# Longer due times in the order planner of a transformer kernel: sums through DRAM, inverses, division

## The chip, the cores and the metric

The kernel runs on one core of one Trainium2 chip. A core has five instruction streams that run in order, each on its own, and meet only at semaphores: PE (TensorE, matmuls, with its weight loads shown apart as PEld), DVE (VectorE), ACT (ScalarE), POOL (GpSimd) and SP (SyncE, which here only issues DMAs). The metric is the device time of one execution in microseconds. Three timed runs of the kernel before took 914.91, 919.50 and 925.57 us, median 919.5 us.

## The reference

The input x is 4 batches of 1,024 tokens with 256 channels, float32. Two layers follow, each added to its input.

```
x = x + attn(layernorm(x))            # 16 heads of 16, causal, ALiBi slopes, then w_proj
x = x + ffn(layernorm(x))
ffn(x): qkv = x @ in_proj.T           # attention over the 4 batches at one position, 16 heads
        h   = layernorm(x + attn @ out_w.T)
        e   = max(top2(softmax(h @ router_w.T)))   # one of 8 experts for each token
        return layernorm(h + gelu(h @ w1[e].T + b1[e]) @ w2[e].T + b2[e])
```

The softmax of the first layer is what this case is about: exp(scores) is multiplied with the values, a column of ones beside the values gives the sum of the exponentials, and the product has to be divided by that sum before the projection w_proj.

## The kernel before, in words

**Attention.** The queries are cut into 20 units (`units`, line 680 on). Units 0 to 11 are 256 queries of one batch each (chunks c = 0, 1, 2 for the four batches in turn), units 12 to 15 the seventh 128 of the queries of each batch, units 16 to 19 the eighth. For every unit four groups g of four heads are worked on in rounds over up to 512 columns of keys: `score` (scores on PE, exponentials on ACT, causal mask on POOL) and `weigh` (product with the values on PE, copied or added into the tile `yt`). There are 160 rounds; two rounds make a slot, so there are 80 slots.

**The way to the division.** The product comes out with channels on partitions, four heads to a tile, and row D of each head holds the sum. To bring sums and values into a shape in which one instruction divides, they go through DRAM: `weigh` writes `yt` to `y` (a DMA); `load_sums(u)` reads the sums back to 128 partitions; `invert(u)` takes their reciprocals on DVE and writes them to `r`; `load_y(u)` issues four DMAs that read `r`, repeated over the 16 channels of each head, into `su`, and the values into `yc`; `divide(u)` multiplies the two on DVE; `project(u)` multiplies with w_proj on PE, and DVE adds the result to x. All DMAs here but those of units 0 to 3's `y` are issued on SP's queue, as are the loads of keys (`fill_slots`), which wait until PE has read what they overwrite. `yc`, `su` and `inverse` have two buffers each. The last unit, 19, goes another way (`normalise`, `project_slots`) without DRAM.

**The second layer.** `front(i)` does all of it up to the routing for 128 positions of all four batches (i = 0 to 7); it may start when `project` of batch 3 has done its queries (`projected`: units 3, 7, 11 give fronts 0 to 5 in pairs, unit 15 gives front 6, the end of attention front 7). At most two fronts run at once during attention, in small steps that fill the space between rounds. When six fronts are placed, `tabulate_first` makes the first table: which tokens go to which expert in 18 tiles of 128. After attention the planner of the tail mixes front 7 (steps marked `last`) and what is left of the others with the tiles of the first table (`tile_step`: gather on POOL, two matmul stages, layernorm, scatter on POOL); then `tabulate_rest` makes the table of the other 20 tiles, and these are done.

**What sets the order.** The program is written out by a planner that keeps a model clock for PE, DVE and ACT (`time`, `busy`, `on_tensor`). Each slot p emits: scores of a round, `E_slot(2p)`, `D_slot(p)`, scores of the next round, the product of an earlier pair of rounds, `E_slot(2p+1)`. An E slot emits work without matmuls, a D slot work with matmuls. When the last product of unit u has been emitted, `attended(u, at)` puts the five steps on lists with the model time at which each is due, `at` plus a constant. An E or D slot pops what is due by PE's model time; so a step is never emitted inside its due time, but in the first slot that begins after it, and several steps that have come due are emitted together. The model clock knows nothing of DMAs, of waits between engines or of the granted clock: it gives the attention phase some 575 model us. At the end of attention whatever is still on the lists is emitted at once, ahead of `normalise(2)`, `normalise(3)`, `project_slots` and the tail.

The constants and where they are used (line 76; `attended`, line 2125, uses them):

```
SUMS_BY, INVERTED_BY, Y_BY, DIVIDED_BY, PROJECTED_BY = 3.0, 6.5, 9.0, 13.0, 14.0
```

The helper at line 587 emits every instruction of PE, DVE and ACT, so most rows carry L587; they are told apart by tile names. PSUM banks are shared between steps, so the matmuls of `project` appear under the names op, xtp, qkp, passed and router, always with the input wp,yc.

Of the kernel before, what the change touches and what calls it, by code (L numbers as in the profile page):

```python
# [72 lines left out]
D_SLOT = 10.0  # L73
SWITCH, COLUMN, EXP_AT_ALL, EXP, READ = 0.2, 1 / 600, 0.17, 1 / 1200, 0.7
AHEAD, EARLY_BY, ROOT, OF_D = 1.0, 0.2, 1.4, 0.35
SUMS_BY, INVERTED_BY, Y_BY, DIVIDED_BY, PROJECTED_BY = 3.0, 6.5, 9.0, 13.0, 14.0

EXP_ZERO = -126 * math.log(2.0)

# [2395 lines left out]
```

## Time and profile before

| | |
|---|---|
| profiled execution | 919.38 us, span 917.7 us from first to last instruction, granted PE clock 0.908 |
| busy in the span | PE 736.4 (80%), PEld 550.0, DVE 545.4 (59%), ACT 416.7, POOL 251.9 us |
| attention, some 40 to 730 us | 80 slots |
| first and last `divide` | 77.0 us, 728.2 us |
| tail, 730 to 918 us | PE busy 139.8, DVE 131.3, POOL 104.6 us |

A row of the trace names the engine, the instruction, the tiles written and read (out<-in), and the time; the views of waits give, for each pair, the idle time of an engine before an instruction and what ended it. "Stretch" tables give the busy time of every engine in one window. Timelines give the start, the duration and, in brackets, the idle time of the engine just before. SPq is SP's sequencer, which issues DMAs; a row there is the issue, not the transfer.

### The profile page before, as it was taken

How to read it: one execution, taken by the hardware profiler on the slowest of the kernel's cores; microseconds unless marked ns; L12 is line 12 of the kernel's file. 1: busy time of each engine (PE TensorE's matmuls, PEld its weight loads, DVE VectorE, ACT ScalarE, POOL GpSimd, SP SyncE). 2: the span in 40 equal slices, each digit the busy share in tenths (PEclk: the TensorE clock that was granted, in tenths of full speed). 3: DMA queues.
4: the chain of work that ended last, by engine and by line, in shares of the span. 5: the costliest groups of instructions: out<-in, count | busy, mean ns of one | idle time of the engine just before them, and what ended most of it. 6: DMA issues, size and time to landing. Idle time of an engine off the chain costs nothing. (4 is left out here: it accounts for less than half of the span.)

```text
span 917.7 us, 22503 instructions
## 1 busy us (share of the span) xinstructions
PE 736.4 (80%) x8917; PEld 550.0 (60%) x8917; DVE 545.4 (59%) x1316; ACT 416.7 (45%) x625; POOL 251.9 (27%) x360
## 2 busy tenths in 40 slices
PE   3995656987999989898886597987798889766983
PEld 2674444655656655565565565776576758655872
DVE  7433313665468767749745435477366768975763
ACT  1452333545446545545553445456346536222540
POOL 5441101212112211212211101012112324508885
PEclk9898778998999999999897898999799989878997
DMA  7444231433325322414252515337242282314430
GB/s 199 137 128 136 74 119 53 122 115 113 98 64 168 93 76 70 143 28 147 67 150 67 161 45 159 93 78 185 62 134 69 76 317 67 108 34 127 119 110 28
DMA packets 75219, 99.56 MB, mean 108 GB/s; under 512 B 19496, under 2 KB 58723, under 8 KB 74596
## 3 DMA queue, kind: packets, MB, share of 16 engines
q1 hardware_dynamic: 64576, 79.63, 29.3%
q0 software_dynamic: 4864, 14.16, 5.1%
q10 hardware_dynamic: 5668, 4.25, 1.5%
q8 instruction: 73, 1.20, 0.6%
q14 instruction: 38, 0.31, 0.1%
HBM read 61.55 MB, written 35.12 MB: 105 GB/s over the span
## 5 line engine op out<-in xcount | busy, mean ns | idle before, releaser
L587 ACT ACTIVATE p<-sk 128x1024 f32<-128x1024 f32 (+1 forms) x320 | 287.6, 939 | 229.3 <-PE sk L587 204.8
L986 POOL TENSOR_SCALAR_AFFINE_SELECT p<-p 128x512 f32<-128x512 f32 (+1 forms) x160 | 104.1, 655 | 505.6 <-ACT p L587 504.0
L587 PE MATMUL sk<-slots 32*128 32x128 f32 (+1 forms) x3456 | 184.9, 333 | 32.2 <-issue 11.0
L587 PEld LDWEIGHTS sk<-slots 32*128 32x128 f32 x3456 | 139.9, 192 | 79.5 <-issue 35.5
L587 PE MATMUL pv<-p,v 128*32 128x128 f32 (+1 forms) x3456 | 151.4, 324 | 8.4 <-ACT p L587 6.5
L587 PEld LDWEIGHTS pv<-p,v 128*32 128x32 f32 x3456 | 100.6, 114 | 48.6 <-issue 14.5
L587 DVE TENSOR_TENSOR yc<-yc,su 128x512 f32<-128x512 f32 (+1 forms) x19 | 11.4, 598 | 116.5 <-DMA yc<-y 116.5
L587 PE MATMUL qkvp<-w_in,ut 128*128 128x264 f32 (+1 forms) x224 | 76.5, 477 | 0.0
L587 PEld LDWEIGHTS qkvp<-w_in,ut 128*128 128x128 f32 x224 | 39.6, 190 | 27.0 <-issue 22.3
L587 PE MATMUL oe<-w,ge 128*128 (+1 forms) x152 | 44.0, 414 | 14.3 <-DVE given L587 6.0
L587 PE MATMUL op<-wp,yc 128*128 128x256 f32 x60 | 21.2, 500 | 42.0 <-DVE yc L587 31.2
L587 PE MATMUL qkp<-xt,wqk 128*128 128x256 f32 x208 | 51.7, 392 | 0.2 <-ACT p L587 0.2
L587 PE MATMUL hid<-mt,w 128*128 128x128 f32 x304 | 48.5, 298 | 3.5 <-DMA w<-in_w_dram 3.1
L1813 POOL DMA_INDIRECT given<-rows,rows x38 | 42.6, 1120 | 23.9 <-DVE at_t L587 13.9
L587 PEld LDWEIGHTS hid<-mt,w 128*128 128x128 f32 x304 | 43.3, 206 | 5.2 <-DMA w<-in_w_dram 3.4
L587 PEld LDWEIGHTS qkp<-xt,wqk 128*128 128x128 f32 x208 | 37.5, 189 | 9.7 <-issue 3.0
L1929 POOL DMA_INDIRECT out_dram<-o,out_rows x38 | 39.0, 1025 | 8.7 <-issue 6.1
L587 PEld LDWEIGHTS op<-wp,yc 128*128 128x128 f32 x60 | 13.5, 243 | 46.4 <-issue 32.2
L587 DVE TENSOR_TENSOR pr<-qkv 128x1024 f32<-128x1024 f32 x32 | 40.2, 1256 | 1.3 <-ACT qkv L587 1.3
L587 DVE TENSOR_TENSOR pv<-qkv,sc 128x1024 f32<-128x1024 f32 x32 | 40.4, 1263 | 0.1
L587 DVE COPY qkv<-qkvp 128x264 f32<-128x264 f32 x28 | 12.0, 431 | 47.3 <-PE qkvp L587 47.3
L587 DVE TENSOR_REDUCE sc<-pr 128x64 f32<-128x1024 f32 x32 | 39.0, 1220 | 1.1
(339 smaller groups left out, 1087.3 us busy)
## 6 DMA issues: line engine op xcount, KB each, us to landing
slots<-k SPq DMA_DIRECT2D x128, 80.0 KB
k<-kq SPq DMA_DIRECT2D x32, 256.0 KB
v<-v SPq DMA_DIRECT2D x16, 288.0 KB
v<-v SPq DMA_DIRECT2D x4, 1152.0 KB
x<-in_x_dram SPq DMA_DIRECT2D x16, 256.0 KB
y<-yt SPq DMA_DIRECT2D x16, 256.0 KB
rows<-x SPq DMA_DIRECT2D x32, 128.0 KB
slots<-k SPq DMA_DIRECT2D x64, 64.0 KB
```

The costliest lines, as they stand in the source:

```text
L587: ins = made(*args, **kwargs)
L986: nc.gpsimd.affine_select(blocks, blocks, pattern=[[0, 2], [0, size], [1, P]], compare_op=ALU.is_ge, fill=0.0, base=0, channel_multiplier=-1,)
L1813: nc.gpsimd.indirect_dma_start(out=self.hx, out_offset=None, in_=t.rows_of, in_offset=bass.IndirectOffsetOnAxis(ap=t.rows_[:, self.j:self. ...
L1929: ins = nc.gpsimd.indirect_dma_start(out=out.rearrange("t n c -> (t n) c"), out_offset=bass.IndirectOffsetOnAxis(ap=t.table.out_rows[:, t. ...
```

## The change

Five constants of the planner get larger. Nothing is added to the computation and nothing removed; the same functions are called with the same arguments, and the same instructions are emitted in another order.

```
-SUMS_BY, INVERTED_BY, Y_BY, DIVIDED_BY, PROJECTED_BY = 3.0, 6.5, 9.0, 13.0, 14.0
+SUMS_BY, INVERTED_BY, Y_BY, DIVIDED_BY, PROJECTED_BY = 7.0, 14.0, 18.0, 29.0, 31.0
```

Since `projected` puts the fronts on the queue, these also can start later.

## The prediction

> **What bounds the kernel now.** I read the page's busy times first, then the waits, then the timelines of one unit. PE is the busiest engine. With matmuls and weight loads merged, it is idle for 115 us between 60 and 730 us of the span and for 32 us in the tail (my union of the trace's records). So in attention it counts what PE waits for. The waits of DVE and PE (us in total, times, longest):
>
> ```profile
> DVE yc L587 <- DMA yc<-y: 116.5, 18, 14.5
> DVE inverse L587 <- DMA sums<-y: 45.6, 12, 7.4
> PE op L587 <- DVE yc L587: 31.2, 4, 9.3
> PE qkp L587 <- DVE yc L587: 17.7, 2, 12.9
> ```
>
> DVE stands still 162.1 us in 30 waits for the DMAs on the way to the division, and PE stands behind it. Unit 12 shows how; timelines of SP, DVE and PE:
>
> ```profile
> 517.87 0.37 SPq L1053 DMA_DIRECT2D r<-inverse  x1
> 520.53 0.60 SPq L1068 DMA_DIRECT2D su<-r  x1
> ...
> 522.44 0.57 SPq L1071 DMA_DIRECT2D yc<-y  x1
> ```
>
> ```profile
> 515.95 0.25 DVE L587 RECIPROCAL inverse<-sums 128x16 f32<-128x16 f32 x1
> 524.91 0.42 DVE L587 TENSOR_TENSOR yc<-yc,su 128x256 f32<-128x256 f32 x1 [8.71 <-DMA yc<-y]
> ```
>
> ```profile
> 515.00 1.17 PE L587 MATMUL sk<-slots 32*128 32x128 f32 x32
> 525.44 2.04 PE L587 MATMUL op<-wp,yc 128*128 128x256 f32 x4 [9.26 <-DVE yc L587]
> ```
>
> The division is DVE's very next instruction after the reciprocal: the model had passed 6.5, 9 and 13 us in one jump of its clock, and all three steps came out together. The real chain is r's issue and landing (517.87 to 520.53), four issues (to 523.01), 1.9 us of landing. PE has `project` next and waits 9.26 us. Adding up where PE's idle time overlaps these waits of DVE gives **74.6 us** of the 115; the rest is spread over keys, exponentials and copies.
>
> A second cost is the clock. Stretches, columns: length, then busy time (and instructions) of PE, PEld, DVE, ACT, POOL, then PEclk, DMA share, GB/s:
>
> ```profile
> 65.00:150.00 85.00, 49.55 (x496) 37.00 (x496) 23.19 (x64) 27.34 (x42) 13.05 (x20) 0.80 0.36 106
> 150.00:250.00 100.00, 90.03 (x906) 62.00 (x907) 58.06 (x120) 50.38 (x71) 21.63 (x27) 0.94 0.35 101
> 250.00:350.00 100.00, 90.96 (x912) 58.69 (x915) 68.37 (x160) 49.41 (x66) 19.04 (x21) 0.95 0.33 101
> ```
>
> Where the long waits lie, the clock is lowest. The trace's clock intervals are at full or half rate; PE works 64.3 us inside half-rate intervals that lie at these waits, and its 128x256 matmul of `project` takes 379 ns at best and 765 ns at worst.
>
> **What the change does, part by part.** It adds and removes no instruction; only places change. To find them I followed the planner's own sums for the kernel before (order, no chip time) and looked up, with the new constants and the same slot times, where each step falls; the new order moves those slot times a little.
>
> *Sums and reciprocal.* Before, 8 of 19 units emit `load_sums` and `invert` in one E slot; with 7 and 14, 2 do (units 3 and 12). Their wait is priced at 45.6 / 12 = 3.8 us of DVE. The other 17 have at least one round between; the 1.7 us from issue to reciprocal in unit 4 (175.8 to 177.5) fits there.
>
> *Reciprocal to division.* `invert` and `load_y` still fall together in 8 units, but then only SP waits, for r to land (2.7 us above); behind SP stand the loads of keys for the next unit, wanted a whole unit later. `load_y` and `divide` fall in one slot in 5 units before and in none after; 11 model us lie between, and attention runs 1.2 real us for each (690 / 575), so some 13 us against 2.6 us of issue and 2 to 4 us of landing (unit 4: last issue 181.3, division 185.7). So DVE finds its data there. What hides the way now is one to three rounds of attention; without that cover it is again 9 us a unit.
>
> *PE's idle time.* Of the 74.6 us I take 65: the two units that coincide keep up to 3.8 each, and PE will find another wait behind some of the others. Bounds 45 (4 in 10 of the gaps turn into waits for copies, such as the 47.3 us that DVE itself waits for qkvp) and 75.
>
> *The clock.* Between 0 and 32 us (half of 64.3). Some half-rate intervals at 290, 311 and 434 us have no long wait, so I take 15. The Trainium skill, TensorE: Matmul & The Clock Gate, section "Part 1: The HAM clock gate", says the ramp penalty is under 1% of a typical kernel's span; by it this term would be 9 us at most and the forecast 6 us later.
>
> *The end of attention.* Before, unit 18's division was emitted in the last E slot and waited 2.07 us at 728.17. Now `attended` at 546.9 of 562.8 model us puts `invert` in the last E slot and `load_y`, `divide` and `project` behind the last round, at once. Behind `divide` on DVE are two `normalise` and the add to x, behind `project` on PE the last projection and the tiles. From reciprocal to `project` unit 12 took 9.2 us, of which the last products cover some 2: **+7 us** (0 to 9).
>
> *Fronts.* `project` of units 3, 7, 11 and 15 moves from slots 11, 28, 51 and 69 to 14, 31, 54 and 71, so the fronts start 2 or 3 slots later. Front 6 and the first table are then 2 or 3 slots less far when attention ends. What stays for the tail, from the rows: about four pairs of pr and sc (1.26 + 1.22 us each) and the softmax between (about 2.6 us), so 12.5 us of DVE, with perhaps the table's last step. DVE is busy 81.54 of 100 us at 730 to 830, where it would lie, so between nothing and 12.5 us, and up to 12 more for the table; I take **+10 us**. Tiles of the first table start later by as much, and these fill PE beside front 7.
>
> *Buffers.* Units come at least 12 model us apart, so `load_y` of unit u+2 comes 42 or more after `attended(u)`, behind `project(u)` at 31 to 39: two buffers suffice nearly everywhere, at no cost.
>
> *Sum*, against the profiled execution's 919.4 us (1.7 over its span, and 0.1 under the median of the runs): 919.4 - 65 - 15 + 7 + 10 = 856.4, so **856 us**.
>
> **The rivals.**
> - *Half the gain.* PE's gaps go, but DVE's work that stood behind them then collides with the copies out of PSUM, which PE waits for; the clock gives nothing. For: DVE is 68% busy at 250 to 350. Against: it is 59% over the span and loses 162 us of waits. 919 - 40 + 7 + 10 = 896 us. Chance 0.16.
> - *A dearer tail.* The first table is not ready when attention ends, so no tile is gathered ahead and the first ones wait for weights behind the layer's. +35 instead of +10 in the tail: 881 us. For: the table's five steps came in slots 75 to 77 of 80, so three slots later touches the end. Chance 0.17.
> - *Cheaper.* The full 75, 30 from the clock, and a tail that takes the rest beside front 7: 919 - 75 - 30 + 7 + 3 = 824 us. Chance 0.12.
> - *Slower.* The fronts slip more than the slots say, so that the table starts only in the tail. Then the 13 tiles that the tail does beside front 7 come behind it, at POOL's 1.12 + 1.03 + 0.75 us each (gather, scatter, root), 38 us, and all of front 6 with its some 40 us of DVE, +7: 85 us against 80 of gain, and with the last of front 5 some 930 us. It decides if fronts slip by five slots or more; I count 2 or 3. Chance 0.06.
> - *Nothing happens*, because the slots are so coarse that the steps come out together as before. The count of slots says no: 0 of 19 divisions in the slot of their loads. 919 us. Chance 0.03.
>
> **How the numbers follow.** Forecast 856 us (840 to 872) has 0.46. The range goes from the cheaper case to half the gain with a few us to spare: 822 to 903. A measurement of this kernel can tell about 1% from no change. Faster by more than 1%: 0.46 + 0.16 + 0.17 + 0.12 = 0.91; within 1%: 0.03; slower: 0.06.
>
> **What will show it.** In the profile after, DVE's waits for yc's and sums' DMAs fall from 162 us to under 30, PE's waits for yc to under 10, and PEclk at 65 to 150 us rises over 0.90. The last `divide` comes at 650 to 670 us instead of 728 and has several us of idle time before it. From it to the end are 190 to 210 us (189.5 before), with more of pr, sc and the table in it. I am wrong if PE's idle time stays above 80 us in attention, or if the tail grows by more than 35 us.

## The result, and the profile after

The changed kernel takes 837.26 us (834.96 to 839.94, 4 runs) against 919.25 us before: a ratio of 0.910, 95% interval 0.904 to 0.917. Measured again beside other kernels it was 0.914 (0.911 to 0.917). The forecast was 856 us, with 822 to 903 as its range. The result lies inside that range, 19 us below the forecast and 3 us below the narrower band of 840 to 872.

The page of the changed kernel, its first lines and the granted clock by slice:

```profile
span 837.1 us, 22503 instructions
...
PE 719.4 (86%) x8917; PEld 540.2 (65%) x8917; DVE 544.6 (65%) x1316; ACT 416.6 (50%) x625; POOL 251.1 (30%) x360
...
PEclk9799889998999999998999999999997699978997
```

The number of instructions is the same and DVE's busy time nearly so (545.4 us before). PE is 17 us less busy (736.4 before) with the same matmuls. The waits that the prediction showed, in the profile after (us in total, times, longest):

```profile
DVE inverse L587 <- DMA sums<-y: 40.9, 8, 11.0
...
DVE yc L587 <- DMA yc<-y: 28.2, 7, 8.6
...
PE op L587 <- DVE yc L587: 5.8, 1, 5.8
...
PE router L587 <- DVE yc L587: 5.2, 1, 5.2
```

The wait for yc has gone from 116.5 to 28.2 us; one more of 5.1 us before a division is put down by the view to a load of keys. PE's wait for the division, in four rows 31.2 + 17.7 + 7.6 + 7.2 us before, is two waits: 5.8 us at the end of attention and 5.2 us at unit 1. The wait for the sums is nearly what it was; more on that below. Unit 12 again, timelines of SP, DVE and PE of the changed kernel:

```profile
461.20 0.38 SPq L1053 DMA_DIRECT2D r<-inverse  x1
461.67 3.27 SPq L939 DMA_DIRECT2D slots<-k  x4
465.25 0.60 SPq L1068 DMA_DIRECT2D su<-r  x1
...
467.15 0.57 SPq L1071 DMA_DIRECT2D yc<-y  x1
```

```profile
459.88 0.24 DVE L587 RECIPROCAL inverse<-sums 128x16 f32<-128x16 f32 x1
...
474.74 0.42 DVE L587 TENSOR_TENSOR yc<-yc,su 128x256 f32<-128x256 f32 x1
```

```profile
478.21 1.03 PE L587 MATMUL vp<-wp,yc 128*128 128x256 f32 x4
```

From reciprocal to division it is now 14.9 us instead of 9.0, but DVE works in between, and neither it nor PE's projection has a wait in brackets. The projection's four matmuls take 1.03 us, where they took 2.04 after the 9 us gap.

By stage (my union of the records of matmuls and weight loads, from 40 us on; attention ends with the last product of exponentials and values):

| kernel | attention ends | PE idle in attention | PE busy in attention | tail | span |
|---|---|---|---|---|---|
| before | 727.7 | 116.2 | 571.5 | 190.0 | 917.7 |
| after | 630.0 | 44.4 | 545.6 | 207.1 | 837.1 |
| waits_gone | 615.0 | 31.7 | 543.3 | 188.2 | 803.2 |
| after_waits_gone | 602.0 | 23.0 | 539.0 | 199.9 | 801.9 |
| division_late | 624.6 | 39.4 | 545.2 | 200.2 | 824.8 |
| division_18 | 649.7 | 57.4 | 552.3 | 202.1 | 851.8 |
| all_shifted | 731.7 | 124.0 | 567.8 | 212.1 | 943.8 |
| fronts_late | 747.1 | 138.9 | 568.1 | 208.1 | 955.2 |
| fronts_early | 664.2 | 65.9 | 558.3 | 202.4 | 866.6 |
| sums_early | 624.1 | 41.1 | 543.0 | 205.7 | 829.8 |
| sums_early_end | 625.8 | 40.8 | 545.0 | 199.8 | 825.5 |

The kernels other than before and after are told below. In span, the change saves 80.6 us: 71.8 of PE's idle time and 25.9 of its busy time in attention, less 17.1 that the tail grew.

### The profile page after: what moved, and what is told of

It reads as the page before. It is cut to its first block, busy times and chain, and to the rows that moved or that the text cites. A ratio compares the mean times of both kernels' runs of the same rounds, so it can differ in the third digit from the quotient of the medians.

```text
span 837.1 us, 22503 instructions
## 1 busy us (share of the span) xinstructions
PE 719.4 (86%) x8917; PEld 540.2 (65%) x8917; DVE 544.6 (65%) x1316; ACT 416.6 (50%) x625; POOL 251.1 (30%) x360
## 5 line engine op out<-in xcount | busy, mean ns | idle before, releaser
L587 PE MATMUL sk<-slots 32*128 32x128 f32 (+1 forms) x3456 | 181.7, 328 | 21.2 <-DVE kq L587 10.0
L587 PEld LDWEIGHTS sk<-slots 32*128 32x128 f32 x3456 | 138.1, 188 | 64.9 <-issue 26.8
L587 PE MATMUL pv<-p,v 128*32 128x128 f32 (+1 forms) x3456 | 144.5, 314 | 10.4 <-ACT p L587 4.6
L587 PEld LDWEIGHTS pv<-p,v 128*32 128x32 f32 x3456 | 96.7, 111 | 48.3 <-issue 8.3
L587 PE MATMUL qkvp<-w_in,ut 128*128 128x264 f32 (+1 forms) x224 | 79.1, 489 | 0.0
L587 PE MATMUL qkp<-xt,wqk 128*128 128x256 f32 x208 | 54.4, 407 | 0.2 <-ACT p L587 0.2
L587 PEld LDWEIGHTS qkp<-xt,wqk 128*128 128x128 f32 x208 | 39.6, 200 | 11.1 <-issue 3.3
L587 ACT COPY qkv<-qkvp 128x512 f32<-128x512 f32 (+1 forms) x28 | 15.3, 555 | 58.5 <-PE qkvp L587 43.9
L587 PEld LDWEIGHTS oe<-w,ge 128*128 128x128 f32 x152 | 28.0, 205 | 17.8 <-DVE given L587 5.7
L587 PE MATMUL vp<-wv,xt 128*128 128x256 f32 x128 | 35.3, 423 | 0.0
```

The lines of the kernel that those rows point to most:

```text
L587: ins = made(*args, **kwargs)
```

## The experiments

**What are the waits worth in all?** The order of before, with what makes DVE wait taken away (two places of the edit; the projection then reads `dv`):

```
-        nc.vector.reciprocal(inverse[:, :width], sums[u])
+        nc.vector.reciprocal(inverse[:, :width], minus_half.to_broadcast([P, width]))
...
-        nc.vector.tensor_tensor(yc, yc, su, ALU.mult)
+        nc.vector.tensor_tensor(dv, flat[:, :n], flat[:, :n], ALU.mult)   # flat is wp_sb
```

> The order of the kernel before, instruction for instruction, with all its DMAs, but the reciprocal reads a constant, and the division multiplies parts of the constant tile wp (384 columns in place of 512, 256 for small units) into a tile of its own that the projection reads: neither waits for a DMA. It leaves out the division by the sums. Theory (the 75 us of PE's idle time under DVE's waits, and 15 to 25 us of clock, are all there is): PE idle between 60 us and the end of attention falls from 115 to some 45 us, PE's busy time falls by 15 to 25 us with the same instructions (the clock alone), tail 189 us as before, time 820 to 834 us. Rival (the gaps turn into other waits): PE idle 80 us, 860 to 880 us.

Measured: 806.79 us, a ratio of 0.883 (0.879 to 0.888), 109 us less, more than both theories allowed. The result of this kernel is not the reference's, since it leaves out the division by the sums, and its divisions are a little narrower; the matmuls are the same. Stretches of this kernel from 40 us to the end of its attention, and of the kernel before (columns as in the prediction):

```profile
40.00:615.00 575.00, 542.78 (x7873) 396.66 (x7871) 392.48 (x883) 338.03 (x465) 126.68 (x186) 0.99 0.42 123
```

```profile
40.00:728.00 688.00, 570.82 (x7870) 413.38 (x7869) 392.10 (x882) 338.20 (x464) 124.58 (x184) 0.91 0.35 103
```

The same matmuls in the same order take 28 us less of PE's time, at a clock of 0.99 for 0.91; idle time falls by another 84.5 us, from 116.2 to 31.7; the tail does not move. So 28 of the 112.7 us that attention gained are the clock. The trace's clock intervals bear this out: PE works 74.5 us inside half-rate intervals of attention before and 13.1 in this kernel, and half of the difference is 31 us. It shows too in the matmuls that stand right behind a wait; groups of the kernel before and of this one:

```profile
L587 PE MATMUL op<-wp,yc 128*128 128x256 f32 x60 | 21.2, 500 | 42.0 <-DVE yc L587 31.2 <-ACT p L587 5.8 <-DVE u L587 3.6
L587 PE MATMUL xtp<-wp,yc 128*128 128x256 f32 x32 | 11.2, 509 | 7.6 <-DVE yc L587 7.6
```

```profile
L587 PE MATMUL op<-wp,dv 128*128 128x256 f32 x60 | 17.2, 425 | 4.0 <-DVE dv L587 3.3 <-ACT yt L587 0.7
L587 PE MATMUL xtp<-wp,dv 128*128 128x256 f32 x32 | 7.8, 386 | 0.0
```

**Which of the five constants?** Only the last two late, then all late with the old distances from loads to division:

```
+SUMS_BY, INVERTED_BY, Y_BY, DIVIDED_BY, PROJECTED_BY = 3.0, 6.5, 9.0, 29.0, 31.0     # division_late
+SUMS_BY, INVERTED_BY, Y_BY, DIVIDED_BY, PROJECTED_BY = 7.0, 14.0, 18.0, 22.0, 23.0   # all_shifted
+SUMS_BY, INVERTED_BY, Y_BY, DIVIDED_BY, PROJECTED_BY = 3.0, 6.5, 9.0, 18.0, 19.0     # division_18
```

> Constants 3.0, 6.5, 9.0 as before, 29.0 and 31.0 as after: sums, reciprocal and loads early, only division and projection late. Theory A (PE loses its time because division and projection are emitted with the loads or within a slot of them): DVE's wait for yc falls under 25 us, its wait for the sums stays near 45 us since 8 units still emit read and reciprocal together, but PE does not see it, because the projection stands 22 model us behind; PE's waits for yc under 10 us; time 832 to 850 us, as the changed kernel. Rival B (what counts is that the whole chain starts later behind the last product, when SP's queue has come along): only half the gain, 870 to 890 us.

> Constants 7, 14, 18, 22, 23: the chain starts as late as in the changed kernel, but from loads to division and projection only 4 and 5 model us, as before. Theory A: in 7 units the division is again in the slot of its loads and in most others one E slot behind, so DVE waits 70 to 110 us for yc, PE 40 to 60 us for DVE; 885 to 910 us. Rival B: 840 to 855 us.

Measured: division_late 832.68 us, ratio 0.911 (0.908 to 0.914), the whole gain; all_shifted 947.28 us, 1.037 (1.033 to 1.042), slower than before. Theory A holds and rival B falls in both. But all_shifted lies outside theory A's numbers too (885 to 910 us, 70 to 110 us of DVE's waits): it came out slower than before. Its projections, and with them the fronts, are 9 model us later, which costs time where waits are left (fronts_late below); how much of it that explains was not measured. The waits of all_shifted, and then the only wait on this way that is left among the 60 longest of division_late:

```profile
DVE yc L587 <- DMA yc<-y: 141.9, 17, 14.3
PE op L587 <- DVE yc L587: 39.3, 7, 9.3
...
PE qkp L587 <- DVE yc L587: 36.1, 5, 15.4
```

```profile
DVE inverse L587 <- DMA sums<-y: 65.4, 13, 12.5
```

In division_late DVE stands 65.4 us before reciprocals, more than in the kernel before, and PE idles 39.4 us, less than in the changed kernel. Of PE's idle time from 60 to 625 us only 7.3 lie under these waits. Here they are nearly free. That PE's next need of DVE is mostly far behind the reciprocal is the likely reason.

> Constants 3.0, 6.5, 9.0, 18.0, 19.0: the division 9 model us behind its loads in place of 4, the projection 5 later than before in place of 17. If 9 model us (11 real) cover the loads, waits for yc stay under 30 us, fronts come hardly later, the first table is ready at the end of attention and the tail is 190 to 195 us: 815 to 828 us. If the full 20 model us of division_late are needed, waits for yc are 50 us and more: 840 to 870 us.

Measured: 858.77 us, 0.944 (0.939 to 0.949), by time the second case. DVE waits 38.2 us for yc's loads, and once more 5.3 us that the view puts down to a load of keys, so its waits lie between the two cases. With 4, 9 and 20 model us from loads to division the ratio is 1, 0.944 and 0.911: the longer the distance, the larger the gain. 9 is too short although 9 model us are 11 real ones and from the first load to the division are some 6 (unit 4 before: 179.4 to 185.7). In all these kernels the projection moved together with the division, so what each of the two distances is worth alone was not measured.

**What do later fronts cost?** In the kernel before, and then the changed order without waits:

```
-            queue.extend(front(PC * c + i + k, fact, 1, False) for k in range(size))
+            due_E.append((time["PE"] + 17.0, 0.0, lambda: queue.extend(
+                front(PC * c + i + k, fact, 1, False) for k in range(size)
+            )))
```

> The kernel before, but fronts get on the queue 17 model us after the projection that frees them: the price of the change's later fronts alone, with all waits for the division left as they are. Theory: front 6 and the first table are 2 slots less far when attention ends; the tail grows from 189 to 198 to 205 us, attention loses 5 to 8 us of work, net +3 to +10 us: 922 to 930 us. Rival (a dearer tail, first table not ready): 940 us and more. Rival (the work moved fits beside front 7): 912 to 919 us.

> The changed constants, with the same cut as waits_gone: reciprocal of a constant, division of parts of wp, so neither waits for a DMA (the division by the sums is left out). Beside waits_gone it shows the price of the later fronts when no wait for the division is left on either side. Theory (in fronts_late 19 us came into attention because later fronts leave the waits less covered, and 18 into the tail because front 6 and the first table are less far): without waits attention is 5 to 12 us shorter than in waits_gone (work moved out), the tail 15 to 19 us longer; 808 to 818 us. Rival (later fronts cost attention time by themselves): 830 us and more.

Measured: fronts_late 957.51 us, 1.047 (1.042 to 1.051), by far worse than my theory; after_waits_gone 802.86 us, 0.882 (0.877 to 0.888), the same as waits_gone at 0.883 and a little under its theory. In fronts_late the time is that of the rival with the dearer tail, and its condition is met (the first table is made at 744 to 768 us, behind the end of attention), but the tail holds only 18 of the 42 us. In both kernels the tail grows, by 18.1 and 11.7 us, with 13 and 11 us more of DVE's work in it. They differ in attention. Without waits it loses 13 us along with the work that moved. With waits it grows by 19.4 us: PE's idle time under DVE's waits goes from 74.6 to 93.5 us. So later fronts cost nothing where no wait is left, and 42 us where the waits are left. That the front's steps, which had stood between loads and division, no longer cover the waits is how I read it; which steps of which unit, I have not taken apart.

**Could the fronts be had early and the waits gone?** As division_late, with shorter times where fronts hang on the projection:

```
+        if units[u][0] % B == B - 1 or u == last_unit - 1:
+            late_by = (3.0, 6.5, 9.0, 16.0, 17.0)
```

> As division_late (3.0, 6.5, 9.0, 29.0, 31.0), but the units of batch 3, whose projection lets fronts start, and unit 18 divide at 16 and project at 17. Theory: 8 units of batch 3 and 18 keep waits of some 2 to 4 us each, the other 11 none; fronts come 3 model us later than in the kernel before; tail 190 to 196 us, attention 622 to 632 us; 814 to 828 us, some 10 us under the changed kernel. Rival (what later fronts cost is small beside what short times cost): 835 us and more.

Measured: 870.17 us, 0.954 (0.947 to 0.961). The theory falls twice. The tail is 202.4 us, no shorter than division_late's 200.2: what stays for the tail is not set by when fronts may start alone (division_18, with projections 5 later in place of 17, also leaves 141.9 us of DVE's work there, against 131.7 before and 142.5 after). And the time rises far above division_late's. (The theory counted 8 short units of batch 3; there are four, 3, 7, 11 and 15, and unit 18.) PE's idle time in attention is 26.5 us above division_late's, of which 11.1 lie under DVE's waits for yc and 7.7 more under those for the sums, and PE is busy 13.1 us longer. But of the two long waits for yc only one, 10.3 us, is at a short unit, 11; the other, 7.7 us, is at unit 2, whose times are the long ones. So that the short times cost all of it is not shown. Unit 11 of this kernel, SP and DVE:

```profile
436.77 0.34 SPq L1053 DMA_DIRECT2D r<-inverse  x1
437.20 0.38 SPq L916 DMA_DIRECT2D v<-v  x1
442.82 0.37 SPq L1036 DMA_DIRECT2D y<-yt  x1
443.29 2.07 SPq L939 DMA_DIRECT2D slots<-k  x4
445.46 0.60 SPq L1068 DMA_DIRECT2D su<-r  x1
```

```profile
450.62 0.69 DVE L587 TENSOR_TENSOR yc<-yc,su 128x512 f32<-128x512 f32 x1 [10.30 <-DMA yc<-y]
```

Here the length of the way comes from SP's queue. SP issues r's write at 436.77 and could read it back some 3 us later (r's issue and landing took 2.7 us at unit 12 of the kernel before). But its issues come out in order, and ahead of the loads stands the next unit's y, for which SP waits 5.2 us (ACT has still to copy `yt`), and then four loads of keys. The loads leave 8.7 us after r's write.

**Do the waits for the sums matter, and the chain at the end of attention?** The second kernel has unit 18 alone at 3, 9, 11, 15, 16; after_end_early is the changed kernel with unit 18 alone at the old times.

```
+SUMS_BY, INVERTED_BY, Y_BY, DIVIDED_BY, PROJECTED_BY = 3.0, 14.0, 18.0, 29.0, 31.0   # sums_early
```

> Constants 3.0, 14.0, 18.0, 29.0, 31.0: as the changed kernel, but the sums are read back at 3 in place of 7, so that 11 model us lie between their read and the reciprocal. In the changed kernel DVE still waits 40.9 us for the sums, in division_late 65.4 us. Theory (these waits cost PE little, since its next need of DVE is far behind the reciprocal; what is left of them in PE's idle time is about 8 us): waits for the sums under 15 us, PE idle in attention 35 us in place of 44, time 4 to 10 us under the changed kernel, 0.900 to 0.906 of the kernel before. Rival (waits for the sums cost PE as those for yc did): 25 us and more under it, below 0.885.

> As sums_early, and unit 18 alone at 3, 9, 11, 15, 16, so that no chain is left behind the last round. Theory: 3 to 6 us under sums_early, since the chain's idle time at the end of attention was 5.8 us in PE's wait for unit 18's division in the changed kernel. Rival (tiles and front 7 set the tail, as after_end_early with its ratio of 0.917 suggests): within 3 us of sums_early.

> The changed kernel, but unit 18 alone keeps 3.0, 6.5, 9.0, 13.0, 14.0, so that its division comes out ahead of the end of attention, as before. It prices the chain of reciprocal, r, loads and division that the change moves behind the last round. Theory: 5 to 8 us of PE's idle time at the end of attention go; the tail falls from 207 to some 200 us; 829 to 833 us. Rival (front 7's chain sets the tail, and tiles fill the gap): 835 to 839 us.

Measured: sums_early 0.914 (0.910 to 0.917), the changed kernel beside it also 0.914 (0.911 to 0.917). The waits for the sums are gone (0.8 us), and yc's have grown to 61.7: DVE only stands in another place. 9.0 us of PE's idle time lie under them, and all of it in attention is 41.1 us for 44.8 in that run of the changed kernel. Neither my 4 to 10 us nor the rival's 25. sums_early_end 827.99 us, 0.906 (0.903 to 0.909), 7 us under sums_early, a little beyond its theory, and the lowest ratio of those that compute the whole result (division_late's interval overlaps it); its tail is 199.8 us for 205.7. after_end_early gives 0.917 (0.912 to 0.922), no gain against 0.910 and 0.914, although its tail is also shorter, 201.5 us; it was not run beside the changed kernel. The two don't agree, so the chain at the end is worth 7 us in one and nothing measurable in the other, and its price stays open. Timelines of that chain in the changed kernel, DVE and PE:

```profile
629.12 0.25 DVE L587 RECIPROCAL inverse<-sums 128x16 f32<-128x16 f32 x1
635.29 0.43 DVE L587 TENSOR_TENSOR yc<-yc,su 128x256 f32<-128x256 f32 x1 [5.92 <-DMA yc<-y]
```

```profile
628.07 1.96 PE L587 MATMUL pv<-p,v 128*32 128x128 f32 x64 [2.85 <-DVE count L587]
635.82 2.05 PE L587 MATMUL op<-wp,yc 128*128 128x256 f32 x4 [5.79 <-DVE yc L587]
```

## Why the prediction was right, point by point

- **What bounds the kernel.** Right. Taking away the waits for these DMAs gives 109 us, with the same matmuls in the same order. Two readings were off, and no term rests on them: in the tail PE is idle for 48 us from 730 us to the end of the span, not 32 (that is the idle time up to 900 us), and the slowest 128x256 matmul of `project` takes 796 ns (under the name qkp), not 765.
- **Order by the slots.** Right for what counts: between reciprocal and division DVE now has other work in every unit but 18. Wrong for the sums: I gave two units a wait, and eight have one. The slots tell when DVE and SP get an instruction, not when SP gets through its queue. Unit 2 of the changed kernel, SP and DVE:

```profile
103.30 1.72 SPq L939 DMA_DIRECT2D slots<-k  x4
...
108.12 0.55 SPq L1045 DMA_DIRECT2D sums<-y  x1
```

```profile
113.31 0.35 DVE L587 RECIPROCAL inverse<-sums 128x32 f32<-128x32 f32 x1 [10.99 <-DMA sums<-y]
```

  DVE is there at 102.3 and waits; SP reads the sums at 108.1, behind loads of keys and the loads for unit 1's division. That division is DVE's next instruction, and PE's 5.2 us at unit 1 come from here: the one place where a wait for sums costs PE several us. So "DVE's waits fall under 30 us" was wrong: 69 us are left, 75 with the one put down to keys. PE feels little of them: 13.2 us of its idle time lie under them, 5.3 of these behind the end of attention. Its waits for yc, forecast under 10 us, are 11.0.
- **PE's idle time, -65.** It fell by 71.8 us. If 8.7 of this go with the later fronts (31.7 to 23.0 in the two kernels without waits), the waits gave 63. Read directly, PE's idle time under these waits of DVE fell from 74.6 to 13.2 us, by 61. About as forecast.
- **The clock, -15.** PE's busy time in attention fell by 25.9 us; 4.3 of it is work that moved to the tail (543.3 to 539.0 in the same two kernels), so the clock gave some 22. By the clock intervals it is 26: PE works 74.5 us at half rate in attention before and 23.4 after. This term was mis-sized, within its bounds of 0 and 32: the 15 that I took, because three half-rate intervals had no long wait, was too low. In waits_gone it is 28 us. The Trainium skill, TensorE: Matmul & The Clock Gate, section "Part 1: The HAM clock gate", puts the ramp penalty under 1% of a typical kernel's span; here 28 of 917.7 us are 3%. The measurement decides: in the kernel before the granted clock fell to half at 16 places between 60 and 730 us, not once at its start.
- **The end of attention, +7.** The tail grew by 17.1 us, and 11.7 of these are the later fronts' (next point), which leaves 5.4; beside the same order without waits it is 207.1 for 199.9, 7.2 us. About as forecast, though the two attempts to take it out don't agree.
- **Fronts, +10.** This term was mis-sized. The tail did grow by 11.7 us, but attention shrank by 13.0 as the work left it: without waits the sum is -1.3 us. I had counted where the work goes to and not where it comes from. With the waits left the same delay costs 42 us (fronts_late), so this price holds only where they are gone.
- **A dearer tail.** The condition of this rival came true: the first table is made at 628 to 656 us, behind the end of attention, and no tile is gathered ahead. Its price, +35, did not: after_waits_gone, with the same late table, is no slower.
- **Last division and tail.** I said 650 to 670 us for the last division; it came at 635.3. From there to the end are 201.8 us, within the 190 to 210 I gave. The clock at 65 to 150 us rose from 0.80 to 0.92, as forecast.

With these sizes the sum is 919.4 - 63.1 - 21.6 + 5.4 - 1.3 = 838.8 us, against 839.3 of the profiled execution. That the two agree is no test, since the terms are shares of the measured 80.6 us; how these are split rests on the two kernels without waits. By this split, of the some 17 us between the sum and the forecast the fronts' term made 11 and the clock's 7. These two erred to the same side, so the forecast is not near by errors that cancel: its largest term, the idle time, was sized well.

## What to carry to other kernels

An engine's wait costs what the bounding engine idles under it, and what that engine then loses at a lower clock, not what the waiting engine itself loses. Under division_late's 65 us of DVE before reciprocals PE idled for 7.3 us; under the 162 us before reciprocals and divisions of the kernel before it idled for 74.6, and without them the kernel took 109 us less. It has to be looked up each time: in fronts_early PE idled for 15 us under 68 us before reciprocals. When a round trip through DRAM is scheduled by hand, set the distance from the last load to the instruction that needs it, not the start of the chain, and reckon with the place of the loads in the issuing queue: at unit 11 of fronts_early that cost more than r's landing. An idle time of PE of several us can be paid twice: in the kernel before, 12 of the 16 stretches at half rate between 60 and 730 us came in or within 5 us behind an idle time of PE under such a wait, and the matmuls behind them took longer (2.04 us for 1.03 in unit 12).

## What the runs showed that I had not expected

- Moving only the start of the second layer's work back by 17 model us made the kernel before 42 us slower, and cost nothing in a kernel without the waits. The work that fills gaps could not be priced apart from the gaps themselves.
- Shifting the whole chain later, with its old distances, made it 3.7% slower (waits for yc 141.9 us for 116.5), so starting later was no help by itself.
- The clock's share of what the waits cost: 28 us of the 113 that attention gained in waits_gone, with the same matmuls in the same order.
